# A planner's cost model learns that VectorE and GpSimd exclude each other at an SBUF port

## The chip, the cores and the metric

The kernel runs on one core of a Trainium2 chip. A core has five engines, each with its own queue that runs in order: TensorE (PE, matrix products; its weight loads are shown as PEld), VectorE (DVE), ScalarE (ACT), GpSimd (POOL) and SyncE (SP, which issues most of the DMAs). SBUF is the core's working memory of 128 partitions, PSUM the small memory that TensorE writes. The metric is device time in microseconds; lower is better.

## The reference

Eight texts `x[b]` (512 x 256, float32) each pass a gated cross-attention block over a context of 1024 x 192, and then a mixture-of-experts feed-forward block. Cut to what matters:

```python
def _L0_xattn_ref(x_text, x_vision, ...):          # T = 512, D = 256, 4 heads of 32
    scores = einsum('bthd,bghd->bhtg', x_text @ Wq, x_vision @ Wk) / sqrt(32)
    topv, topi = top_k(scores, 32)                 # of 1024 keys
    attn = zeros.at[..., topi].set(softmax(topv))
    c_t = einsum('btg,bgd->btd', attn.mean(axis=1), x_vision @ Wv)
    x = layernorm(x_text) ; x = x * (1 + gate * scale_in(c_t)) + gate * shift_in(c_t)
    y = s4d(x, ...)                                # long convolution, by FFT
    y = y * (1 + gate * scale_out(c_t)) + gate * shift_out(c_t)
    xt = x_text + y
    xt = xt + gelu(layernorm(xt) @ W1 + b1) @ W2 + b2
    return layernorm(xt)

def _L0_ffn_ref(x, ...):                           # 8 experts, one per token
    top_id = argmax(x @ gate_w) ; xs = x * sigmoid(max(x @ gate_w))
    routed = the chosen expert's (silu(xs @ rt_gate) * (xs @ rt_up)) @ rt_down
    return swiglu(x, sh_gate, sh_up, sh_down) + routed

x = x + tanh(g_xattn) * xattn(layernorm(x), ctx) ; x = x + tanh(g_ffn) * ffn(layernorm(x))
```

## The kernel before

**The work.** For each text, `prepare` loads `x` and the context and makes keys `kT` and queries `qT`. `attention` walks over 4 tiles of 128 rows times 2 pairs of heads, 64 steps for the eight texts. For each head TensorE makes the scores (`pS`, in PSUM), ACT copies them to `sc`, and VectorE finds the 32 largest of 1024 by a fold into `mn` and `hi` (maxima and minima of pairs, two int32 additions on GpSimd), then rounds of `max` (8 values, into `top`) and `match_replace` (which strikes them out). ACT makes exponentials `e`, VectorE masks them (`scalar_tensor_tensor`, `e<-sc,t,e`), ACT scales them, and GpSimd adds them over the heads into `acc`. TensorE transposes `acc` (`pa`) and multiplies it by the context (`pu`). `mixed` does the modulation and the convolution by a discrete Fourier transform written as matmuls (`pxf`, `yf`, `py`), `after_mix` the two-layer network (`pm`, `am`), the norms and the shared expert (`p`, `ae`). Rows are scattered by expert to a table in DRAM (`xtab`), and `block` later takes 128 rows of one expert at a time (`pg`, `pu`, `pyr`), adding its result to the output with an accumulating DMA that GpSimd issues. `setup` makes the convolution's spectrum once, from elementwise work on `ta`, `tk`, `tp`, `qa`, `qk`, `qq`.

**How it is staged.** While attention works on text b, `mixed`, `after_mix` and some routed blocks of text b - 1 (or `setup`, for the first) and `prepare` of text b + 1 stand beside it. After the last attention come the last text's feed-forward work and the remaining blocks.

**The order is planned.** The program's operations are not issued as they are written. Proxies of the engines (`Plan.engine`) record each one as an `Op`: its engine, `dur` (time from start to result), `cost` (time that the engine is taken), `lat` for a DMA, and what it reads and writes. `order` (L267) then runs up to 8 passes for each of three phases of TensorE's clock window: `forward` (L303) is a list scheduler that always takes, over all engines, the operation that can begin first, and among those of one engine the one with the lowest rank; `backward` gives new ranks from the latest possible starts; `timed` (L370) computes a made order's time for every phase. The order with the smallest summed time is issued, all five queues at once. `begun` (L289) says when an operation's engine is free and when its result is there; `time` (L176) holds the durations by engine, method and width; `after` has the hops between engines. Buffers are part of the plan: a tile waits for the one that it replaces.

Before the change, an operation's duration does not depend on what other engines do, except for TensorE's clock and the DMAs' shared wire.

Of the kernel before, what the change touches and what calls it, by code (L numbers as in the profile page):

```python
# [12 lines left out]
F32 = mybir.dt.float32  # L13
# [7 lines left out]
PSUM = bass.MemoryType.PSUM  # L21
# [21 lines left out]
AGAIN = {"PE": 0.0, "DVE": 0.034, "ACT": 0.032, "POOL": 0.08, "SP": 0.0}  # L43
OVERLAP = {"DVE": 0.083, "ACT": 0.1, "POOL": 0.04, "SP": 0.0}
DRAIN, REFILL, LOAD = 0.163, 0.095, 1.41
TABLES = {"Exp": "e", "Tanh": "e", "Gelu": "g", "Silu": "s", "Sin": "t"}


class Op:
    __slots__ = ("i", "eng", "fn", "cost", "lat", "table", "acc", "succ", "npred", "est", "tiles", "end", "start", "what", "k", "dur")  # L50


class Clock:
# [21 lines left out]
class Plan:  # L75
# [49 lines left out]
    def note(self, eng, method, fn, args, kw, cost=None):  # L125
        aps = [v for v in list(args) + list(kw.values()) if hasattr(v, "tensor") or hasattr(v, "tag_meta")]
        out = kw["out"] if "out" in kw else args[0]
        outs = [out] + [kw[k] for k in ("accum_out",) if kw.get(k) is not None]
        ins = [v for v in aps if not any(v is o for o in outs)]
        for k in ("in_offset", "out_offset"):  # L130
            if kw.get(k) is not None:
                ins.append(kw[k].ap)
        dma = "dma_start" in method
        whole = kw.get("out_offset") is not None
        op = Op()
        op.eng, op.fn, op.what = eng, fn, (method, getattr(getattr(out, "tensor", out), "name", "?"))
        op.table = None
        n = 1
        for k in list(out.shape)[1:]:
            n *= k  # L140
        op.lat = None
        if dma:
            moved = out if kw.get("out_offset") is None else kw["in_"]
            size = self.width(moved) * list(moved.shape)[0] * 4
            op.cost = op.dur = 0.42 if eng != "POOL" else 1.07
            op.lat = (2.9 if "indirect" not in method else 2.4) + size / WIRE
            if kw.get("compute_op") is not None:
                op.lat += 2.0
        else:
            op.dur, op.table = self.time(eng, method, out, outs, ins, args, kw, n)  # L150
            op.cost = op.dur - DRAIN if eng == "PE" else max(op.dur - OVERLAP[eng], 0.02)
        self.add(op, ins, outs, whole)

    def note_products(self, parts):

        op = Op()
        op.eng, op.table, op.lat, op.cost, op.dur = "PE", None, None, ROWS_COST, ROWS_COST + DRAIN
        op.what = ("matmul", getattr(getattr(parts[0][0], "tensor", parts[0][0]), "name", "?"))

        def run():  # L160
            for out, lhs, rhs in parts:
                self.nc.tensor.matmul(out, lhs, rhs, start=True, stop=True)  # L162

        op.fn = run
        self.add(op, [v for p in parts for v in p[1:]], [p[0] for p in parts])

    def note_dma(self, eng, fn, out, ins, whole=False):
        if not self.noting:
            return fn()
        op = Op()  # L170
        op.eng, op.fn, op.table, op.cost, op.dur = eng, fn, None, 0.9, 0.9
        op.what = ("dma", out.tensor.name if hasattr(out, "tensor") else out.name)
        op.lat = 2.9 + self.width(out) * P * 4 / WIRE
        self.add(op, ins, [out], whole)

    def time(self, eng, method, out, outs, ins, args, kw, n):  # L176

        f = None
        if eng == "ACT" and method == "activation":
            f = TABLES.get(str(args[2]).split(".")[-1])  # L180
        width = max([n] + [self.width(v) for v in ins])
        points = sum(1 for v in ins if self.width(v) == 1) if width > 1 or method == "activation" else 0
        psum = any(getattr(v, "space", None) == PSUM for v in ins + [out])
        if eng == "PE":
            if method == "transpose":
                return 0.109 + DRAIN, None
            lhs = args[1]
            two = lhs.dtype == F32
            t = max(n * (2 if two else 1) / 2400 + 0.0017, 0.018 + 0.00042 * self.width(lhs))
            return (2 if two else 1) * t + DRAIN, None  # L190
        if eng == "DVE":
            if method == "memset":
                return 0.1, None
            if method == "reciprocal":
                return 0.15 + 0.00627 * n, None
            t = 0.146 + width / 960
            if method in ("tensor_scalar", "tensor_copy") and not psum and out.dtype == F32:
                t = 0.146 + width / 1920
            if method in ("match_replace", "max_index"):
                t += 0.08  # L200
            if method in ("tensor_scalar", "scalar_tensor_tensor"):
                t += 0.055 * min(points, 1)
            if len(outs) > 1:
                t += 0.02
            return t, None
        if eng == "ACT":
            t = (0.157 if psum else 0.187) + n / 1200
            if method == "activation":
                t += 0.1 * (points - (1 if n == 1 else 0))
            return t + (0.092 if len(outs) > 1 else 0), f  # L210
        if eng == "POOL":
            if kw.get("op") == ALU.pow or (len(args) > 3 and args[3] == ALU.pow):
                return 1.045, None
            if method in ("memset", "iota"):
                return 0.1 + 0.0008 * n, None
            if method in ("tensor_scalar", "tensor_copy"):
                return 0.22 + 0.002 * n, None
            return 0.19 + 0.0021 * n, None
        return 0.4, None
# [47 lines left out]
    def order(self):  # L267

        best = None
        for phase in PHASES:  # L270
            rank, switch = [o.k for o in self.ops], SWITCH
            for _ in range(PASSES):
                run = self.forward(rank, switch, phase)
                worth = sum(self.timed(run, p) for p in PHASES)
                if best is None or worth < best[0]:
                    best = worth, run
                rank, switch = self.backward(run), WAIT
        self.total, (done, _, _, _) = best[0] / len(PHASES), best[1]
        return done

    def after(self, o, st, en, fin, s):

# [3 lines left out]
            return fin + HOP[s.eng]  # L286
        return st if o.eng == "PE" else fin + AGAIN[o.eng]

    def begun(self, o, st, free, clock, wire):  # L289

        cost = o.cost
        if o.eng == "PE":
            if st > free + 0.05:
                cost += REFILL
            end = clock.run(st, cost)
            return end, end + DRAIN, end + DRAIN, wire
        end = st + o.dur
        if o.lat is None:
            return st + cost, end, end, wire
        wire = max(end, wire) + max(o.lat - 2.9, 0.0)  # L300
        return st + cost, end, max(end + o.lat, wire + 2.9), wire

    def forward(self, rank, switch, phase):  # L303

        ops, n = self.ops, len(self.ops)
        free = {e: 0.0 for e in ("PE", "DVE", "ACT", "POOL", "SP")}
        clock, table, wire = Clock(phase), None, 0.0
        left = {t: len(v[1]) for t, v in self.tiles.items()}
        last = {t: 0.0 for t in self.tiles}
        slots = {id(q): [(0.0, None)] * q[0] for q in self.queues.values()}  # L310
# [3 lines left out]
        done, start, end = [], [0.0] * n, [0.0] * n  # L314
        est, need = [0.0] * n, [1 + o.npred + len(o.tiles) for o in ops]
# [22 lines left out]
        while len(done) < n:  # L338
            best = None
# [12 lines left out]
            if e == "ACT" and o.table not in (None, table):  # L352
                st, table = st + LOAD, o.table
            start[o.i] = st
            free[e], en, fin, wire = self.begun(o, st, free[e], clock, wire)
            end[o.i] = fin
            done.append(o)
            for i in o.succ:
# [11 lines left out]
    def timed(self, run, phase):  # L370

        done, _, _, before = run
        free = {e: 0.0 for e in ("PE", "DVE", "ACT", "POOL", "SP")}
        clock, table, wire, total = Clock(phase), None, 0.0, 0.0
        est, last = [0.0] * len(done), {t: 0.0 for t in self.tiles}
        for o in done:
            e = o.eng
            st = max([free[e], est[o.i]] + [last[before[t]] + 0.06 for t in o.tiles if before[t] is not None])
            if e == "ACT" and o.table not in (None, table):
                st, table = st + LOAD, o.table  # L380
            free[e], en, fin, wire = self.begun(o, st, free[e], clock, wire)
            total = max(total, fin)
            for i in o.succ:
                est[i] = max(est[i], self.after(o, st, en, fin, self.ops[i]))
            for t in o.tiles:
                last[t] = max(last[t], fin)
        return total
# [1268 lines left out]
```

## Time and profile before

| | us |
|---|---|
| median of 3 runs | 1596.76 |
| lowest, highest | 1593.42, 1599.82 |
| the profiled execution | 1599.94 |
| its span, first to last instruction | 1598.2 |
| busy: TensorE, VectorE, ScalarE, GpSimd | 1376.2, 1212.5, 1110.2, 939.0 |
| mean granted TensorE clock (1 is full speed) | 0.898 |

A row of the profile names engine, operation and tiles (out <- in, buffer numbers left out), the shapes, how many there are, and times. Nearly all instructions carry one source line (L465, the place where the plan issues them; the score products have L162), so they are told apart by their tiles. A row of waits reads: engine and tile that waited <- what ended the wait: total us, how often, the longest. A row of a stretch gives the length, then each engine's busy time and count, TensorE's granted clock, the DMA engines' busy share and GB/s. An operation that waits for an engine's port after it was issued shows as a longer operation, not as a wait.

### The profile page before, as it was taken

What the parts mean: (1) busy time and instruction counts of PE and PEld (TensorE: products, weight loads), DVE (VectorE), ACT (ScalarE), POOL (GpSimd) and SP (SyncE); (2) the same over time, 40 slices, a digit from 0 to 9 for tenths busy, and PEclk for the clock granted to TensorE, in tenths of its full rate; (3) what the DMA queues carried; (4) which work ended last, traced back from release to release, by engine and by line L of the source; (5) the groups of instructions that cost most, each with busy time, mean ns of one, the idle gap of its engine ahead of it and who ended that gap; (6) DMA issues with size and microseconds to landing.
All of it is one profiled execution on the core that took longest, in us unless ns stands there. A gap on an engine that the chain in (4) does not pass through costs nothing. (4 is left out here: it accounts for less than half of the span.)

```text
span 1598.2 us, 21011 instructions
## 1 busy us (share of the span) xinstructions
PE 1376.2 (86%) x6321; PEld 854.0 (53%) x6321; DVE 1212.5 (76%) x3077; ACT 1110.2 (69%) x1988; POOL 939.0 (59%) x1070
## 2 busy tenths in 40 slices
PE   6355689887997998999999988999999899889885
PEld 2133344454554454756466545754665377547784
DVE  7999999988996898879968995799679953313110
ACT  7687966897678858977798769776977676024121
POOL 6688857646574765664757574767475746314122
PEclk8555579796999798989999999999999899989998
DMA  4000010010201120333014401450144026535691
GB/s 132 1 14 14 24 54 20 14 53 21 80 14 53 29 77 14 122 103 112 14 62 127 149 14 44 129 165 14 54 122 142 0 84 203 192 129 168 188 274 29
DMA packets 99929, 129.98 MB, mean 81 GB/s; under 512 B 9479, under 2 KB 72156, under 8 KB 99806
## 3 DMA queue, kind: packets, MB, share of 16 engines
q1 hardware_dynamic: 91886, 119.34, 22.9%
q0 software_dynamic: 6864, 8.41, 3.0%
q8 instruction: 52, 0.85, 0.2%
q10 hardware_dynamic: 1056, 0.79, 0.2%
q14 instruction: 71, 0.58, 0.1%
HBM read 110.52 MB, written 18.65 MB: 81 GB/s over the span
## 5 line engine op out<-in xcount | busy, mean ns | idle before, releaser
L465 POOL TENSOR_TENSOR acc<-acc,e 128x1024 f32<-128x1024 f32 x96 | 229.0, 2386 | 127.2 <-ACT e L465 103.7
L465 DVE MAX8 top<-mn 128x8 f32<-128x256 f32 (+1 forms) x512 | 262.5, 546 | 1.5 <-POOL mn L465 0.7
L162 PE MATMUL pS<-kT,qT 32*128 32x512 f32 x512 | 187.5, 721 | 63.3 <-DVE mn L465 37.9
L465 DVE SCALAR_TENSOR_TENSOR e<-sc,t,e 128x1024 f32<-128x1024 f32 x128 | 185.3, 1461 | 32.5 <-ACT e L465 32.3
L465 ACT COPY sc<-pS 128x512 f32<-128x512 f32 x256 | 140.0, 583 | 94.2 <-PE pS L162 64.1
L465 DVE TENSOR_TENSOR mn<-sc,pS 128x512 f32<-128x512 f32 x256 | 167.6, 676 | 36.5 <-PE pS L162 23.2
L465 POOL TENSOR_TENSOR mn<-mn 128x256 int32<-128x256 int32 x128 | 109.2, 857 | 100.6 <-DVE hi L465 89.7
L465 ACT ACTIVATE e<-sc,sm 128x1024 f32<-128x1024 f32 x128 | 145.6, 1147 | 19.3 <-POOL acc L465 18.4
L465 ACT ACTIVATE junk<-sc,sm 128x1024 bf16<-128x1024 f32 x128 | 146.2, 1142 | 0.7
L465 PE MATMUL pu<-aT,cx 128*96 128x128 f32 x1024 | 134.1, 282 | 10.4 <-ACT aT L465 10.3
L465 PEld LDWEIGHTS pu<-aT,cx 128*96 128x96 f32 x1024 | 121.5, 168 | 36.4 <-issue 21.1
L465 PE MATMUL pm<-hT,w 128*128 128x512 f32 x256 | 130.9, 655 | 8.2 <-ACT hT L465 8.2
L465 ACT ACT_TABLE_LOAD x101 | 129.6, 1283 | 7.9 <-DMA xt<-in_x_dram 6.2
L465 PE MATMUL am<-w,ga 128*128 128x256 f32 x512 | 121.9, 386 | 12.0 <-ACT ga L465 11.9
L465 ACT ACTIVATE e<-e,sm 128x1024 f32<-128x1024 f32 x96 | 107.8, 1143 | 21.8 <-DVE sm L465 21.7
L162 PEld LDWEIGHTS pS<-kT,qT 32*128 32x128 f32 x512 | 50.6, 203 | 134.4 <-DVE mn L465 54.0
L465 PEld LDWEIGHTS am<-w,ga 128*128 128x128 f32 x512 | 96.0, 192 | 42.6 <-ACT ga L465 20.6
L465 POOL TENSOR_TENSOR yf<-yf,t 128x512 f32<-128x512 f32 (+1 forms) x80 | 90.1, 1150 | 33.2 <-DVE t L465 32.5
L465 POOL TENSOR_TENSOR mn<-mn,hi 128x256 int32<-128x256 int32 x128 | 104.6, 821 | 3.8
L465 DVE MATCH_REPLACE8 mn<-top,mn 128x256 f32<-128x256 f32 x256 | 103.7, 408 | 0.0
L465 PEld LDWEIGHTS pm<-hT,w 128*128 128x128 f32 x256 | 52.3, 211 | 67.1 <-issue 50.2
L465 DVE TENSOR_REDUCE hi<-mn 128x256 f32<-128x512 f32 x128 | 86.5, 682 | 0.0
(305 smaller groups left out, 2993.4 us busy)
## 6 DMA issues: line engine op xcount, KB each, us to landing
w<-in_L_xattn_W_dram SPq DMA_DIRECT2D x32, 512.0 KB
rt_gate<-in_L_ffn_rt_gate_dram SPq DMA_DIRECT2D x29, 512.0 KB
rt_up<-in_L_ffn_rt_up_dram SPq DMA_DIRECT2D x29, 512.0 KB
rt_down<-in_L_ffn_rt_down_dram SPq DMA_DIRECT2D x29, 512.0 KB
cx<-in_ctx_dram SPq DMA_DIRECT2D x7, 768.0 KB
xtab<-zt SPq DMA_DIRECT2D x8, 642.5 KB
xt<-in_x_dram SPq DMA_DIRECT2D x8, 512.0 KB
xo<-in_x_dram SPq DMA_DIRECT2D x8, 512.0 KB
```

The source lines that it names most:

```text
L162: self.nc.tensor.matmul(out, lhs, rhs, start=True, stop=True)
L465: o.fn()
```

## The change

Only the planner is changed; the operations, their operands and their DMAs are the same, and the order in which they are issued is planned anew.

- Each `Op` has a flag `port`. It is set for every GpSimd operation that is not a DMA, and for a VectorE operation that has two or more inputs wider than one element per partition outside PSUM, or that is a `tensor_scalar` or `tensor_copy` from SBUF to a float32 output in SBUF.
- `begun` keeps, for VectorE and GpSimd, until when its last flagged operation runs. A flagged operation of the other engine that starts before that, less `HEAD` = 0.15 us, is lengthened by what is left, in `cost` and `dur`. `forward` and `timed` share this; the choice of the next operation in `forward` is as before.
- A DMA that GpSimd issues with an accumulation is given 1.57 us in place of 1.07.
- The time of a matmul has as its lower bound, for the weights' load, 0.003 + 0.00085 per column in place of 0.018 + 0.00042 per column.
- The best run is kept as `self.run`; the wire's state moves into the same dictionary as the two ports' (`held`).

```diff
+HEAD = 0.15
...
-            op.cost = op.dur = 0.42 if eng != "POOL" else 1.07
+            op.cost = op.dur = 0.42 if eng != "POOL" else 1.57 if kw.get("compute_op") is not None else 1.07
...
+            wide = sum(self.width(v) > 1 and v.space != PSUM for v in ins)
+            fast = method in ("tensor_scalar", "tensor_copy") and wide and PSUM != out.space and out.dtype == F32
+            op.port = eng == "POOL" or eng == "DVE" and (wide > 1 or fast)
...
-            t = max(n * (2 if two else 1) / 2400 + 0.0017, 0.018 + 0.00042 * self.width(lhs))
+            t = max(n * (2 if two else 1) / 2400 + 0.0017, 0.003 + 0.00085 * self.width(lhs))
...
-    def begun(self, o, st, free, clock, wire):
-
-        cost = o.cost
+    def begun(self, o, st, free, clock, held):
+
+        cost, dur = o.cost, o.dur
         if o.eng == "PE":
             if st > free + 0.05:
                 cost += REFILL
             end = clock.run(st, cost)
-            return end, end + DRAIN, end + DRAIN, wire
-        end = st + o.dur
+            return end, end + DRAIN, end + DRAIN
+        if o.port:
+            wait = max(0.0, held["DVE" if o.eng == "POOL" else "POOL"] - st - HEAD)
+            cost, dur = cost + wait, dur + wait
+            held[o.eng] = st + dur
+        end = st + dur
         if o.lat is None:
-            return st + cost, end, end, wire
-        wire = max(end, wire) + max(o.lat - 2.9, 0.0)
-        return st + cost, end, max(end + o.lat, wire + 2.9), wire
+            return st + cost, end, end
+        held["wire"] = max(end, held["wire"]) + max(o.lat - 2.9, 0.0)
+        return st + cost, end, max(end + o.lat, held["wire"] + 2.9)
```

## The prediction

> **What bounds the kernel now.** I read the page's busy shares and slices first, then the sums over three stretches, then TensorE's waits in each, and last the rows of the operations that the change speaks of.
>
> ```profile
> PE 1376.2 (86%) x6321; PEld 854.0 (53%) x6321; DVE 1212.5 (76%) x3077; ACT 1110.2 (69%) x1988; POOL 939.0 (59%) x1070
> ...
> PE   6355689887997998999999988999999899889885
> ...
> DVE  7999999988996898879968995799679953313110
> ...
> POOL 6688857646574765664757574767475746314122
> ```
>
> The 40 slices (40 us each) show three stages. In the first ten VectorE is near 9 and TensorE far below; then TensorE stands at 8 to 9 with VectorE close behind; in the last six VectorE is nearly idle. The sums over the same stretches (columns PE, PEld, DVE, ACT, POOL busy, then granted clock):
>
> ```profile
> 0.00:400.00 400.00, 277.97 (x1307) 149.65 (x1308) 373.11 (x837) 308.08 (x553) 277.71 (x268) 0.73 0.11 34
> 400.00:1340.00 940.00, 881.59 (x3897) 541.88 (x3896) 790.16 (x2105) 748.70 (x1333) 594.27 (x709) 0.96 0.25 78
> 1340.00:1598.00 258.00, 216.61 (x1121) 162.44 (x1119) 49.22 (x136) 53.44 (x103) 66.99 (x95) 0.93 0.53 166
> ```
>
> VectorE bounds the first 400 us (373 of 400; TensorE idle 122 us, at a granted clock of 0.73). TensorE bounds the next 940 us (882 busy, 58 idle, clock 0.96). The last 258 us hold no attention, and the chain that ended last runs there through TensorE; the change has next to nothing to act on in them. TensorE's waits in the first stretch, then in the second:
>
> ```profile
> PE pS L162 <- DVE mn L465: 37.9, 11, 9.3
> PE pz L465 <- POOL tp L465: 17.7, 3, 9.6
> PE pS L162 <- ACT sc L465: 16.2, 5, 7.1
> ```
> ```profile
> PE hT_p L465 <- ACT hh L465: 14.3, 5, 6.5
> PE am L465 <- ACT ga L465: 11.1, 6, 3.1
> PE pS L162 <- ACT sc L465: 8.9, 3, 4.5
> ...
> PE py L465 <- POOL yf L465: 3.8, 4, 1.3
> ```
>
> Early, 56 us of TensorE's waits end directly with VectorE or GpSimd; in the long middle stage hardly 7 us do. Last, the operations in question (count: shortest, median, longest in ns):
>
> ```profile
> L465 DVE SCALAR_TENSOR_TENSOR e<-sc,t,e x128: 1246/1280/4317, 41.3 to 1324.3; 128x1024 f32<-128x1024 f32 x128
> ...
> L465 POOL TENSOR_TENSOR acc<-acc,e x96: 2342/2364/3351, 48.8 to 1331.6; 128x1024 f32<-128x1024 f32 x96
> ```
> ```profile
> L465 DVE MATCH_REPLACE8 mn<-top,mn x256: 397/408/550, 36.2 to 1322.0; 128x256 f32<-128x256 f32 x128
> ...
> L465 POOL TENSOR_TENSOR mn<-mn,hi x128: 715/728/1723, 32.1 to 1318.8; 128x256 int32<-128x256 int32 x128
> ...
> L465 DVE MATCH_REPLACE8 mn<-top,hi x128: 397/406/426, 34.2 to 1317.9; 128x256 f32<-128x256 f32 x128
> ```
>
> The exclusion is real for the masking step `e<-sc,t,e` (both operands in SBUF): its work is 1.28 us, but it can take 4.32. It is not there for `match_replace`, which hardly varies although GpSimd is busy 63% of the middle stage. In one place the trace has one beside GpSimd: the sum `acc` ran from 715.82 to 718.18 us, and `match_replace` began at 715.97 and took 0.40.
>
> **The change part by part.** Nothing is added to or taken from the chip's work; every instruction and DMA may move, SP's and GpSimd's queues included, because all five orders come from the passes. So the costs are of two kinds: what the planner now believes, and what the order it then picks costs.
>
> (1) True exclusion. The stretch in the first 400 us, by the rows of that stretch, count times (mean minus a clean duration of the same shape): mask 34 x (1557 - 1280) = 9.4 us; `qa<-qa,qk` 8 x (2054 - 1215) = 6.7; `qq<-qq,qk` 8 x (1642 - 1215) = 3.4, the 1215 being the row `yf<-pxf,kf` with an operand in PSUM; `tk<-tk,ta` 8 x (1597 - 681) = 7.3 and `ta<-ta,tk` 8 x (1363 - 681) = 5.5, the 681 being `t<-pxf,kf`; `tensor_scalar` into `tk` and `qk`, against their shortest (401 and 676), 8 x 594 + 8 x 305 = 7.2. Sum 39.5 us, in the stage that VectorE bounds. In the middle stage the mask's is 94 x (1427 - 1280) = 13.8 us, and GpSimd's `mn` pair 92 x (836 - 728) + 92 x (787 - 728) = 15.4 us, both beside a busy TensorE. What can this give? `forward` still takes the operation that can begin first; the wait only lengthens it after it was chosen. Nothing steers around a conflict; the gain is that ranks, and the choice among 3 x 8 orders, rest on truer times. Ends: all of 39.5 saved, or nothing. I take a fifth, 8 us, nearer the low end because of that; a reshuffle could also add conflicts, so the low end is not a floor. The middle stage I put at nothing: TensorE covers it; with that cover gone it would be the 13.8 us.
>
> (2) False exclusion. The test counts inputs wider than one element. `match_replace` has two (the 8 values `t8` and the source), so all 384 are marked, though the rows above show no stretch. In the middle stage there are 276. Low end of what the planner will charge: only the first of each head, which starts one `max` (0.41 us) after GpSimd's `mn` addition of 0.73 has begun, so 92 x (0.73 - 0.41 - 0.15) = 16 us. High end: each one meets GpSimd at its busy share, 0.63, and waits half of what runs: acc 170.8 us of 594 in pieces of 2.37, the rest taken at 1.0, so (170.8 x 1.19 + 423 x 0.5) / 594 - 0.15 = 0.55 us; 276 x 0.63 x 0.55 = 96 us. Middle: 56 us. In the planner's eyes VectorE then carries 790 + 56 = 846 us (at the high end 886) beside TensorE's 882: two bounds in place of one. It will believe that attention needs products `pS` later than it does, and put other matmuls ahead of them; TensorE's queue is in order, so `mn` waits on `pS` (20.3 us in this stage now), and behind `mn` on VectorE stand the maxima, the mask, and then ACT's `acc` and TensorE's transposes. Later in the image TensorE runs out of the work it pulled forward and waits for attention. What of the 56 us becomes time is not in the trace: none at one end (VectorE has 940 - 790 = 150 us of slack there), all 96 at the other. I take a third of 56, 18 us, nearer none because of the slack.
>
> The Trainium skill, page "VectorE: DVE Perf Modes", section "Two Vector instructions with no wait between them", treats a match-value load with a match-replace as two instructions of one input each; and "SBUF — State Buffer", section "Who interferes with whom", says that a VectorE instruction with at most one SBUF input outside the two-port modes does not contend with GpSimd. By these pages the mark on `match_replace` is wrong, as the row of 397/408/550 says; had it been a true two-input case, term (2) would be nothing and the sum 8 us of gain.
>
> (3) The accumulating DMA's issue, 1.07 to 1.57: its row has a median of 1645 ns, so this is truer. Of 37, 19 lie in the middle stage: 19 x 0.5 = 9.5 us of GpSimd time now foreseen, beside TensorE. I cost it at nothing, between -9.5 and +9.5. (4) The weight load's bound: for 128 columns a pass of a narrow matmul goes from 0.1084 to 0.1118 us. `pg`, `pu`, `pgo`, `puo` are 1184 passes, 4 us in all in the planner's eyes; the gate's 128 passes go from 0.072 to 0.112, 5 us. Nothing on the chip changes; the bounds are -9 and +9 us of misplaced matmuls, taken at nothing. (5) ACT loads its tables 101 times at 1.28 us; a new order may have some more or fewer: ten are 13 us of ACT, which had 191 us idle in the middle stage, so nothing. (6) `self.run` and the tidied returns cost nothing.
>
> Sum: 18 - 8 = +10 us. The profiled execution took 1599.94 us (span 1598.2), 3.2 above the median of 1596.76; with +10 it would be 1609.9, and as a median 1607.
>
> **The rivals.** *A, the truer times win (faster).* The first 400 us tighten: three fifths of the 39.5 us stretch goes, 24 us, and the false waits cost under half of my 18, say 8: 1597 - 24 + 8 = 1581. For it: the conflicts there sit on the bounding engine, and TensorE loses 56 us to VectorE and GpSimd. Against it: the greedy choice does not avoid a conflict. It decides when (1) saves more than (2) costs; at 18 us that means nearly half of the stretch. *B, hidden anyway.* TensorE is at 94% for 940 us, both terms cancel: 1597 within 8. Included here is that the change doesn't do what it says: the stretched rows keep their length and the order is only shuffled. *C, VectorE's false load becomes the plan's bound.* Half of the high end, 48 us, less 8: 1637. For it: 886 against 882 in the planner's eyes; against it: VectorE's slack.
>
> **How the numbers follow.** About 0.5% (8 us) is what a measurement of this kernel can tell from no change. My forecast (slower by 4 to some 25 us) has 0.36, A 0.38 with its cases from -8 to -32 us, B 0.14, C 0.12. A is a wide bundle on the other side; the single likeliest sign is slower: forecast and C together, less the 0.02 of the forecast inside 8 us, give 0.46; same 0.16; faster 0.38. The time is 1607; its own range is 1601 to 1622. Leaving out a tenth at either end, the range runs from 1568 (somewhat past A's value) to 1637 (C's).
>
> **What would show it.** Right: the middle stage's TensorE idle grows beyond 58 us, with more of `mn <- pS` on VectorE, while the first 400 us of work end a little earlier and the rows `qa`, `tk`, `ta` shorten. Wrong: setup's VectorE rows shrink by 20 us or more and the middle stage keeps its 94%; or the mask's mean (1461 ns) and setup's rows grow, so that the plan doesn't do what it says; or the loss lies in table loads or waits on weights' DMAs, which I cost at nothing. `match_replace` should stay at 0.41 us whatever happens.

## The result and the profile after

The changed kernel took 1618.57 us (median of 4 runs, 1616.55 to 1621.63) against 1595.09 us for the kernel before: a ratio of 1.0142, 95% interval 1.012 to 1.0164. It is slower, as forecast, by more than twice the forecast amount (23 us, not 10), and the next sections show that a good part of this came from something that the forecast had no term for.

The page's busy shares of the changed kernel (engine, busy us, share, instructions), to set beside the first fence of the prediction:

```profile
PE 1387.1 (86%) x6321; PEld 859.7 (53%) x6321; DVE 1209.8 (75%) x3077; ACT 1115.0 (69%) x1992; POOL 949.4 (59%) x1070
```

TensorE has the same 6321 instructions and is busy 10.9 us longer. Its mean granted clock fell from 0.898 to 0.890, and 1376.2 x 0.898 / 0.890 = 1388.6: by this ratio the clock alone would make that part. The span grew from 1598.2 to 1616.0, by 17.8 us, so the other 6.9 us are more idle time on TensorE. The sums by stretch (columns as before):

```profile
0.00:400.00 400.00, 274.64 (x1298) 151.95 (x1299) 363.12 (x810) 308.56 (x548) 273.11 (x262) 0.72 0.12 34
400.00:1340.00 940.00, 883.69 (x3818) 536.25 (x3817) 791.71 (x2103) 738.00 (x1316) 594.66 (x699) 0.95 0.25 76
1340.00:1616.00 276.00, 228.80 (x1207) 171.50 (x1206) 55.00 (x166) 68.43 (x129) 81.63 (x111) 0.94 0.53 163
```

In the middle stage TensorE is not idler than before (56 us against 58), but it gets 3818 instructions done in it, not 3897, at a clock of 0.95, not 0.96. In the first 400 us VectorE is idle 37 us, not 27, and has done 810 instructions, not 837. The masks, and the outputs that leave for DRAM (from the views of these tiles: count, shortest, median, longest in ns, first and last start in us):

```profile
L475 DVE SCALAR_TENSOR_TENSOR e<-sc,t,e x128: 1251/1283/4592, 48.9 to 1341.4; 128x1024 f32<-128x1024 f32 x128
```
```profile
L475 SPq DMA_DIRECT2D out_dram<-xr x8: 388/400/432, 417.7 to 1504.9; - x8
```

Before, the last mask started at 1324.3, and the outputs left between 407.5 and 1485.6:

```profile
L465 SPq DMA_DIRECT2D out_dram<-xr x8: 384/396/496, 407.5 to 1485.6; - x8
```

So the delay is 10 us after setup, 17 at the last mask and 19 at the last output. It does not build up evenly: by the trace the 32nd mask starts at 375.0 us (367.4 before), the 64th at 679.7 (677.6), the 80th at 842.5 (826.7). So what setup lost was nearly regained by the end of the fourth text's attention (16 masks each), and lost anew in the fifth.

The rows that the change speaks of hardly got shorter in sum. First the first 400 us of the kernel before (count | busy, mean ns | idle before), then of the changed kernel:

```profile
L465 DVE SCALAR_TENSOR_TENSOR e<-sc,t,e 128x1024 f32<-128x1024 f32 x34 | 52.4, 1557 | 2.4 <-ACT e L465 2.4
...
L465 DVE TENSOR_TENSOR qa<-qa,qk 128x1024 f32<-128x1024 f32 x8 | 16.4, 2054 | 0.0
...
L465 DVE TENSOR_TENSOR qq<-qq,qk 128x1024 f32<-128x1024 f32 x8 | 13.1, 1642 | 0.0
L465 DVE TENSOR_TENSOR tk<-tk,ta 128x512 f32<-128x512 f32 x8 | 12.8, 1597 | 0.0
L465 DVE TENSOR_TENSOR ta<-ta,tk 128x512 f32<-128x512 f32 x8 | 10.9, 1363 | 0.0
```

```profile
L475 DVE SCALAR_TENSOR_TENSOR e<-sc,t,e 128x1024 f32<-128x1024 f32 x34 | 50.1, 1491 | 1.0 <-ACT e L475 1.0
...
L475 DVE TENSOR_TENSOR qq<-qq,qk 128x1024 f32<-128x1024 f32 x8 | 16.6, 2074 | 0.8 <-ACT qk L475 0.8
L475 DVE TENSOR_TENSOR qa<-qa,qk 128x1024 f32<-128x1024 f32 x8 | 14.3, 1791 | 0.0
...
L475 DVE TENSOR_TENSOR ta<-ta,tk 128x512 f32<-128x512 f32 x8 | 13.0, 1624 | 0.0
L475 DVE TENSOR_TENSOR tk<-tk,ta 128x512 f32<-128x512 f32 x8 | 10.4, 1296 | 0.0
L475 DVE TENSOR_SCALAR qk<-qa 128x1024 f32<-128x1024 f32 x8 | 8.1, 1012 | 0.0
L475 DVE TENSOR_SCALAR tk<-ta 128x512 f32<-128x512 f32 x8 | 6.5, 818 | 0.0
```

By the prediction's own sum (count times mean less clean duration): 7.2 + 4.6 + 6.9 + 4.9 + 7.5 + 6.0 = 37.1 us of stretch, against 39.5. `qq`, `ta` and, by a little, the `tensor_scalar` into `qk` (981 to 1012 ns) went up, the other four down.

### The profile page after: what moved, and what is told of

Read it like the earlier page. It is cut to its first block, busy times and chain, and to the rows that moved or that the text cites. A ratio compares the mean times of both kernels' runs of the same rounds, so it can differ in the third digit from the quotient of the medians.

```text
span 1616.0 us, 21019 instructions
## 1 busy us (share of the span) xinstructions
PE 1387.1 (86%) x6321; PEld 859.7 (53%) x6321; DVE 1209.8 (75%) x3077; ACT 1115.0 (69%) x1992; POOL 949.4 (59%) x1070
## 5 line engine op out<-in xcount | busy, mean ns | idle before, releaser
L167 PE MATMUL pS<-kT,qT 32*128 32x512 f32 x512 | 194.1, 748 | 62.5 <-DVE mn L475 45.6
L475 POOL TENSOR_TENSOR mn<-mn 128x256 int32<-128x256 int32 x128 | 103.7, 820 | 119.4 <-DVE hi L475 107.2
L475 PE MATMUL pm<-hT,w 128*128 128x512 f32 x256 | 137.8, 676 | 6.4 <-ACT hT L475 6.0
L167 PEld LDWEIGHTS pS<-kT,qT 32*128 32x128 f32 x512 | 55.3, 210 | 142.8 <-DVE mn L475 66.7
L475 DVE MATCH_REPLACE8 mn<-top,mn 128x256 f32<-128x256 f32 x256 | 103.2, 407 | 0.0
```

What stands on the lines that cost most here:

```text
L475: o.fn()
```

## The experiments

The planner is part of the program, so its account can be read beside the chip's time: for each kernel below, "own total" is the time that its own passes give to the order that they picked (the mean over three clock phases). It is a belief and no measurement; what matters is how it goes with the time measured. The kernel before has an own total of 1496.5, the changed kernel 1549.3. Ratios are against the kernel before, run on the same chip, whose medians were 1597.4 to 1597.9 us.

Reading the flags out of the two plans gave the first surprise. On VectorE, 252 operations are flagged: 128 of `match_replace` and 32 of `max_index`, and none of the 128 masks; of setup's in-place `ta`, `tk` sum, `qa` and `qq`, none either. `note` drops from its inputs whatever is the same object as the output. The mask writes `e` and reads `sc` and `e`, so it counts one wide input: the rule as "The change" puts it holds only for operands that are not the output as well. For the same reason only the first `match_replace` of each head is flagged, whose source is `hi`; the others work in place. In its own order the changed planner charges 57.5 us of waits to `match_replace` and nothing to the masks, out of 117 us in all.

Three theories stood at this point. Theory 1 is the prediction's: the false exclusion of `match_replace` costs the time. Theory 2: the two constants do. Theory 3: the old order was a lucky draw, and any other order of this planner is worse.

**e1: without the false flag.**

```diff
-            op.port = eng == "POOL" or eng == "DVE" and (wide > 1 or fast)
+            op.port = eng == "POOL" or eng == "DVE" and (wide > 1 or fast) and method not in ("match_replace", "max_index")
```

> The changed kernel with match_replace and max_index left unflagged; all else of the change stays. Theory 1 (the false exclusion of match_replace costs the time): about 1595 us, within 8 us of the kernel before, the masks' last start back near 1324 us. Theory 2 (the two constants, 1.57 us for the accumulating DMA and the weight load's bound, do it): about 1618 us, as the changed kernel. Theory 3 (the old order was a lucky draw, and any other order of this planner is some per cent worse): 1605 to 1625 us with no relation to which flag is set.

1604.5 us, ratio 1.0048 (1.0028 to 1.0068); own total 1524.5.

**e2: the false flag alone.** On the kernel after, with the old constants:

```diff
-            op.port = eng == "POOL" or eng == "DVE" and (wide > 1 or fast)
+            op.port = eng == "POOL" or eng == "DVE" and wide > 1 and method in ("match_replace", "max_index")
```

> The kernel before with one thing of the change: match_replace and max_index alone are flagged on VectorE (160 operations, all of GpSimd's as in the change), the constants are the old ones. Theory 1: about 1618 us, the whole loss. Theory 2: about 1595 us. Theory 3: 1605 to 1625 us.

1608.1 us, ratio 1.0053 (1.0026 to 1.0079); own total 1511.0.

**e3: the flag mended.** As e1, and:

```diff
-            wide = sum(self.width(v) > 1 and v.space != PSUM for v in ins)
+            read = [v for v in list(args[1:]) + [kw[k] for k in kw if k.startswith("in")] if hasattr(v, "tensor") or hasattr(v, "tag_meta")]
+            wide = sum(self.width(v) > 1 and v.space != PSUM for v in read)
```

> The changed kernel with the flag mended: inputs that are also the output are counted, so the 128 masks and the in-place setup work are flagged, and match_replace and max_index are not. If knowing the real exclusion helps (rival A's mechanism): below 1587 us. Theory 1: within 8 us of 1595 us or better. Theory 2: about 1618 us. Theory 3: 1605 to 1625 us.

1610.1 us, ratio 1.0084 (1.0062 to 1.0105); own total 1581.4. All 128 masks are flagged now, and it is still slower than before.

**e4: the two constants alone**, no flag (the two lines of the change's diff with 1.57 and 0.00085, on the kernel before).

> The kernel before with the two constants alone (1.57 us for the accumulating DMA, 0.003 + 0.00085 per column for the weight load); no flag at all. Theory 1: about 1595 us, within 8. Theory 2: about 1618 us. Theory 3: 1605 to 1625 us.

1610.5 us, ratio 1.0087 (1.0065 to 1.0109); own total 1512.2.

Four different edits gave 1604 to 1611 us, each slower than the kernel before and faster than the changed one. Theory 1 passes in e1: 1604.5 is 6.6 us above the 1597.9 of the kernel before on that chip, and the last mask starts at 1307.4 us. It fails in e3 and e4, where it asked for about 1595, and in e2, where it asked for the whole loss. Theory 2 asked for 1595 in e2 and 1618 in the others, and fails in all. Theory 3 fits e2, e3 and e4, and e1 lies 0.5 us below its band, so the next runs change nothing that the planner learns: each operation that `note` records has its time to the result (`dur`) changed by at most 0.1%. On the planner of before (j) or of the change (k):

```diff
+        op.dur *= 1 + 1e-3 * math.sin(len(self.ops) * 12.9898 + SEED)
         self.add(op, ins, outs, whole)
```

> The planner of before, in which every operation's believed duration is changed by a fixed pseudo-random share of at most 0.1% (a sine of its number, seed 0); nothing is learned by it. Theory 3 (any new order is worse than the old one, which was a good draw; e1 to e4, four different edits, all came out 0.5 to 0.9% slower): 1603 to 1615 us. Theory 1 or 2 (what the planner knows decides, so a change in the fourth digit does nothing): 1590 to 1602 us.

1601.5 us, ratio 1.0017 (0.9988 to 1.0046); own total 1501.8.

> The same with seed 1. Theory 3: 1603 to 1615 us. Theory 1 or 2: 1590 to 1602 us.

1600.5 us, ratio 1.0012 (0.9993 to 1.003); own total 1497.3.

> The same with seed 2. Theory 3: 1603 to 1615 us. Theory 1 or 2: 1590 to 1602 us.

1593.7 us, ratio 0.9978 (0.9959 to 0.9998); own total 1494.2.

> The planner of the changed kernel with the same pseudo-random change of at most 0.1%, seed 0. Theory 3 alone (the change's planner draws from the same spread as the old one's): 1600 to 1615 us, below the 1618.6 of the change. If the false exclusion has a cost of its own on top of the reshuffling: 1613 to 1625 us again.

1600.2 us, ratio 1.0024 (1.0009 to 1.0038); own total 1537.2.

Theory 3 falls: three reshuffles of the old planner average 1598.6, so the old order was an ordinary draw. But k0 shows something larger than any part of the change: a change in the fourth digit of its durations made the changed kernel 18 us faster. And the own totals run in the order of the times: among the old planner's four, whose times lie close together (the intervals of neighbours overlap), and between k0 and the changed kernel. That gave theories 4 and 5: within one planner the own total tells a bad draw from a good one, or it doesn't. Twenty-four seeds of each planner were planned, and the last runs taken from near their ends (k2's total is the second highest of its 24, t21's the second lowest).

> The planner of the changed kernel with every believed duration changed by at most 0.1%, seed 2. Its own total for the order that it picks is 1552.5 us, near the change's 1549.3; k0's was 1537.2 (the totals are means of the planner's own account over three clock phases). Theory 4 (the change's 1618.6 is one draw out of a spread, and what the planner believes says within one planner which draw is bad): 1610 to 1625 us. Theory 5 (the draw is blind: the changed planner's belief says nothing): 1597 to 1612 us, as k0.

1618.5 us, ratio 1.0129 (1.0101 to 1.0157).

> The same with seed 5, the order for which the changed planner has the lowest total of 24 seeds, 1523.0 us (26 below the change's). Theory 4: 1580 to 1595 us, faster than the kernel before. Theory 5: 1597 to 1612 us.

1588.9 us, ratio 0.9956 (0.9939 to 0.9973).

> The planner of before with seed 7, the lowest total of its 24 seeds: 1482.0 us against 1496.5 for the kernel before. Theory 4: 1580 to 1592 us. Theory 5: 1594 to 1602 us, as j0 to j2.

1589.2 us, ratio 0.9957 (0.9935 to 0.9979).

> The planner with the mended flag (that of e3_true) with seed 21, 1566.4 us by its own total against 1581.4 for e3_true, which took 1610.1 on the chip. Theory 4: 1585 to 1600 us. Theory 5: 1600 to 1615 us. If a planner that knows the real exclusion orders better (rival A's mechanism): below 1587 us.

1597.0 us, ratio 0.9992 (0.9976 to 1.0007).

All four lie in theory 4's bands, and none in theory 5's. Rival A's mechanism got no support: knowing the real exclusion did not bring t21 below 1587 us. All kernels whose planner was tried more than once (the changed kernel's time was taken beside a kernel before of 1595.1 us, the others beside 1597.4 to 1597.9):

| planner | kernel | own total | measured us | difference |
|---|---|---|---|---|
| before | j7 | 1482.0 | 1589.2 | 107.2 |
| before | j2 | 1494.2 | 1593.7 | 99.5 |
| before | the kernel before | 1496.5 | 1597.8 | 101.3 |
| before | j1 | 1497.3 | 1600.5 | 103.2 |
| before | j0 | 1501.8 | 1601.5 | 99.7 |
| changed | k5 | 1523.0 | 1588.9 | 65.9 |
| changed | k0 | 1537.2 | 1600.2 | 63.0 |
| changed | the changed kernel | 1549.3 | 1618.6 | 69.3 |
| changed | k2 | 1552.5 | 1618.5 | 66.0 |
| mended flag | t21 | 1566.4 | 1597.0 | 30.6 |
| mended flag | e3 | 1581.4 | 1610.1 | 28.7 |

Within a planner the belief ranks the orders almost as the chip does (k2 and the changed kernel are level; of the old planner's five only j7 and, barely, j2 are clear of the kernel before), and the difference moves by at most 8 us. Between planners it can't be compared, since each of these two prefers its own order. The changed planner, asked for the kernel before's order, gives it 1578.8, 29 us more than its own; the old planner gives the changed kernel's order 1530.0, 33 us more than its own. The chip sides with the old one, by 21 to 23 us.

Over the 24 seeds the old planner's own totals go from 1482.0 to 1507.5 (mean 1496.3), the changed one's from 1523.0 to 1553.0 (mean 1543.3), the mended one's from 1563.9 to 1583.8 (mean 1574.4). Adding each planner's mean difference gives an estimate of its typical kernel: 1496.3 + 102.2 = 1598 us before, 1543.3 + 66.1 = 1609 us with the change, 1574.4 + 29.7 = 1604 us with the mended flag. So the kernel before was a typical draw of its planner. Of the 21 us between the two in this table, about 11 us come with its planner and about 9 us with a draw in the bad part of its spread (both estimates, 1609 - 1598 and 1618.6 - 1609, each unsure by some us as the differences are; what is measured is that a neighbouring draw, k0, is 18 us faster).

The profiles of the good and the bad draw of the changed planner, k5 and then k2, differ where the changed kernel and the one before do:

```profile
PE 1380.0 (87%) x6321; PEld 858.6 (54%) x6321; DVE 1207.7 (76%) x3077; ACT 1118.3 (70%) x1994; POOL 939.2 (59%) x1070
```
```profile
PE 1395.6 (86%) x6321; PEld 864.8 (53%) x6321; DVE 1212.0 (75%) x3077; ACT 1128.7 (70%) x2002; POOL 944.3 (58%) x1070
```

The spans are 1587.2 and 1617.5. Of these 30.3 us, 15.6 are TensorE busy longer with the same instructions (granted clock 0.894 and 0.888; this ratio alone makes 9 of them) and 14.7 are TensorE idle. The clock is low where TensorE idles (0.71 to 0.74 in the first 400 us of the kernels above, 0.95 to 0.96 in the middle), so an order with more gaps seems to pay twice, by the gap and by the clock; that the gaps lower it is read from these rows, and no run tested it apart.

## Why the prediction was right in its sign, and what of its cause was not found

*The bounds* were read rightly and stayed: VectorE in setup, TensorE after it. The median of 1618.57 lies in the range; the increase is 23 us where 10 was forecast. That it lies there is in good part luck: of the three other orders of the changed planner that were run, k0 (1600.2) and k5 (1588.9, faster than the kernel before, and chosen for its low total) lie below the range of 1601 to 1622, and k2 (1618.5) inside.

*Step (1), true exclusion, 8 us saved.* The stretch went from 39.5 to 37.1 us, so 2.4. The step failed in its reading of the code: it took the masks and the in-place setup rows to be flagged, and they are not. The reason given for a small gain, that the greedy choice does not avoid a conflict, fits e3 and t21: with the flag mended, the orders are not better (typical 1604 by estimate). In e3, where every mask is flagged, the masks took 1474 ns in the mean, and 1461 in the kernel before; the rows before and in e3:

```profile
L465 DVE SCALAR_TENSOR_TENSOR e<-sc,t,e 128x1024 f32<-128x1024 f32 x128 | 185.3, 1461 | 32.5 <-ACT e L465 32.3
```
```profile
L476 DVE SCALAR_TENSOR_TENSOR e<-sc,t,e 128x1024 f32<-128x1024 f32 x128 | 187.2, 1474 | 54.4 <-ACT e L476 54.1
```

*Step (2), false exclusion, 56 us believed and 18 paid.* The planner's charge to `match_replace` is 57.5 us, but the agreement is luck: 128 of 384 are flagged, where the step counted all and priced only the middle stage. They are the ones of the step's low end, which took 0.17 us for each; the planner charges 57.5 / 128 = 0.45. That the exclusion is false for `match_replace` held, for it took as long in the changed kernel as before:

```profile
L475 DVE MATCH_REPLACE8 mn<-top,mn x256: 396/408/420, 37.8 to 1340.2; 128x256 f32<-128x256 f32 x128
...
L475 DVE MATCH_REPLACE8 mn<-top,hi x128: 396/408/420, 36.2 to 1334.6; 128x256 f32<-128x256 f32 x128
```

As for the price, the signs it named are absent. The wait that should have grown in the middle stage, `mn` on `pS`, shrank (waits: total us, times, longest; before, then after):

```profile
DVE e L465 <- ACT e L465: 29.9, 9, 9.0
DVE mn L465 <- PE pS L162: 20.3, 10, 8.4
...
DVE mn L465 <- ACT sc L465: 8.5, 14, 2.0
```

```profile
DVE e L475 <- ACT e L475: 41.5, 17, 10.1
DVE mn L475 <- ACT sc L475: 17.3, 14, 4.7
DVE mn L475 <- PE pS L167: 12.0, 9, 4.4
```

Its waits on `sc`, ACT's copy of the same products, grew by as much, so the two together stayed level (28.8 us, then 29.3); what grew is the masks' wait for ACT's exponentials. TensorE's idle time there is 56 us, not over 58. That this flag costs something on the planner's average is possible (the estimate of 11 us has to come from somewhere), and e1, 14 us faster without it, points that way, but e1 without it and e2 with it alone are one draw each and don't separate it (and the other 92 flags on VectorE were not run alone). Planned with the same 24 seeds, the planners of e1, e2 and e4 have mean own totals of 1521.8, 1522.1 and 1509.9, with 17 to 20 us from lowest to highest. With the one difference known for each (80.0, 97.1 and 98.3) that makes typical kernels of about 1602 us without the flag, 1619 with the flag alone and 1608 with the constants alone. These are estimates from one measured kernel each, and they do not add up. So the flag may cost more than e2 shows (its own total of 1511.0 lies below all of its 24), and it stays open how the 11 us divide between the flags and the two constants.

*Steps (3) and (4), the constants, nothing.* Truer by the rows (the accumulating issue takes 1642 ns in the mean before, and one `pg` product starts 0.111 us after another), and yet e4 with them alone took 1610.5 us, 12.5 more than the kernel before. That is more than either bound, 9.5 and 9 us, and less than the two together; e4 is one draw, and how much of it the constants themselves make is open.

*Step (5), table loads, nothing.* 101 became 105, and 112 in e1, 98 in j7, 115 in k2; k5 has 107 and is fast, e4 has 96 and is slow. They don't decide.

*What the working lacked* is a term for the reshuffle itself. Every edit to this list scheduler's numbers that was tried gave a new order, and the spread of such orders (24 seeds within 20 to 30 us of own total; 1589 to 1619 us on the chip for the orders that were run) is as wide as anything that the edit is about. The rivals had B as "the order is only shuffled" and took that for within 8 us of no change; k2 and k5, which differ in the fourth digit of some durations, are 30 us apart.

## What to carry to other kernels

A change to a scheduler's cost model is judged on several orders of each model and not on one: jitter the costs a little, and compare the spreads. If its own total ranks its orders as the chip does, planning from many jittered starts and keeping the lowest total can be worth more than a truer constant: here j7 and k5 are both 0.4% faster than the kernel before (a small gain, but their intervals end at 0.9979 and 0.9973), with the old model and with the flawed new one, and the truer constants alone were 0.9% slower. And a test on "operands read" should be checked by listing what it flags, in-place operands above all.

## What the runs showed of the hardware that I had not expected

A VectorE operation that waits for the port can be passed over by a whole queue. In k2 one mask took 7.76 us instead of 1.28. VectorE and GpSimd around it (start us, us, engine, line, operation, count):

```profile
1089.65 7.76 DVE L476 SCALAR_TENSOR_TENSOR e<-sc,t,e 128x1024 f32<-128x1024 f32 x1
1097.35 0.08 DVE L476 DVE_READ_ACCUMULATOR e<-sc,t,e 128x1 f32 x1
```
```profile
1088.68 1.84 POOL L476 TENSOR_TENSOR yf<-yf,t 128x512 f32<-128x512 f32 x1
1089.91 1.28 POOL L476 TENSOR_TENSOR mn<-mn 128x256 int32<-128x256 int32 x1
1090.59 4.38 POOL L476 TENSOR_TENSOR yf<-yf,t 128x512 f32<-128x512 f32 x4
1094.41 1.24 POOL L476 TENSOR_TENSOR mn<-mn,hi 128x256 int32<-128x256 int32 x1
1095.09 1.23 POOL L476 TENSOR_TENSOR mn<-mn 128x256 int32<-128x256 int32 x1
```

Eight operations of GpSimd, each starting by its record before the one in front had ended, ran one behind the other from 1088.68 to 1096.32 us, and the mask ended 1.09 us after the last. The mask had begun second of the nine. So here the turn did not go to the one that had waited longest; a GpSimd queue without gaps kept it. The longest masks of the other kernels (4317 ns before, 4592 after) point the same way: in the kernel before, four additions into `xo` ran from 677.48 to 680.79 us beside it. The change's rule lets VectorE wait for one GpSimd operation and then makes GpSimd wait. That is what most places show: of the 474 masks over 1.4 us in the fourteen profiles, 434 ended before any GpSimd operation that had begun after them; 34 were passed over by one, and six by two or more.
